# The joint of two stages: piece order, issuing queue and scale engine in the hand-over from a 7x7 convolution to an MLP

## The chip, the cores and the metric

One NeuronCore of a Trainium2 chip runs the whole kernel. The metric is device time in microseconds (us), as the median of repeated runs; a profiled execution of the same kernel gives the lines shown. Engines: PE is TensorE, DVE is VectorE, ACT is ScalarE, POOL is GpSimd, SP is SyncE, which here only issues DMAs.

## The reference

Two blocks with a residual each, on x of 8 x 96 x 96 x 192 in float32. The second, which the change is about, is a group norm, a 7x7 depthwise convolution, a norm over the 192 channels and an MLP of 192 to 768 to 192.

```python
def reference(x, ...):
    # layer 0: projection to 384, 3x3 depthwise conv, four running means, norm, projection to 192
    x = x + _L0_conv_ref(_gn(x), ...)
    # layer 1
    x = x + _L1_conv_ref(_gn(x), ...)
    return x

def _L1_conv_ref(x, dw_kernel, dw_bias, ln_gamma, ln_beta, w0, b0, w1, b1, gamma):
    y = lax.conv_general_dilated(x, dw_kernel, ...) + dw_bias      # 7x7, one filter a channel
    mu = jnp.mean(y, axis=-1, keepdims=True)
    var = jnp.mean(jnp.square(y - mu), axis=-1, keepdims=True)
    y = (y - mu) * lax.rsqrt(var + EPS) * ln_gamma + ln_beta
    y = jax.nn.gelu(jnp.einsum('bhwc,cd->bhwd', y, w0) + b0, approximate=False)
    return (jnp.einsum('bhwd,dc->bhwc', y, w1) + b1) * gamma
```

## The kernel before

Stages a to c compute layer 0 and leave its result in DRAM as `X1_d`. The change is in the last two stages.

**Stage d, the convolution.** The work is cut into 32 blocks, `todo[n]`: two halves of the batch times 16 groups of 12 channels (`NI` is 16). For a block, `load_raw(n, t)` fetches three tiles (`t` is 0 to 2) of 384 KB twice from `X1_d` (L926), `load_band(n)` fetches the filter bands (L936), `scale_steps(n)` applies the group norm in 24 small steps (`scale`, L951 to L960: on ScalarE or VectorE, by `n` and `t`) and one copy of the band to the other half of the partitions (`spread`, L964). `conv_d(n, c)` does one of six columns: 24 matmuls in the trace (L1337) and two evictions with the bias by ScalarE (L1347). `store_d(n)` writes the block to `Y_d` with six DMAs of SP (L1364 to L1369). The first `N1` = 19 blocks run one after the other in stage d proper ("own" blocks, 0 to 18). The last 13 (19 to 31) are *inlaid*: their steps are put into the slots of stage e.

**Stage e, norm and MLP.** It runs over 36 tiles of rows, `load_y(n)`, each of which gives two *units* u (72 units). A tile comes in 40 pieces: for each of eight partition blocks `q` four main pieces `b` of 60 KB (L1398) and one small piece of 16 KB with the channels of the last group (L1404). `q` below 4 goes to the buffer `ya`, the rest to `yb`; there are two buffers of each, so tile 2 needs the place of tile 0. The norm of a unit is a chain of seven steps, `norm_steps_e(u)`: sums, mean, center, square (ScalarE), squares, powers (a pow on GpSimd, L1508), scale, nearly all of the rest on VectorE. Three transposes (`turn_in`, L1529) hand it to TensorE; `first_layer` (L1544, L1554) and its GELU on ScalarE (L1563), `second_layer` (L1574), the residual add on VectorE (`xo`, L1585) and the output DMA by GpSimd (L1593) follow. `load_r` fetches the residual rows of a tile (1.5 MB, L1419), `bias_r` adds a bias to them on GpSimd (L1425).

**Order.** All of it is written out by hand: each engine executes its instructions in the order in which the program names them. In the own blocks the loop over `n` names: loads of block n + 2, store of block n - 1, `steps`, the six columns (with two pieces of tile 0 after each, on ScalarE's queue, in blocks 12 to 14: `main_y`), then `on_scalar` and `rest_y`. Tile 0's other pieces are named at the end of block 16 (`NI`), tile 1 at the end of block 17. The chain of unit 0 begins in block 17, that of unit 1 in block 18. In the loop over units the chain of unit u + 2 and the rest of unit u + 1's are named between the parts of unit u; `slot()` is called five times a unit, and names one slot of inlaid work and up to 14 pieces of a tile that is being loaded. A tile n + 2 is loaded from the end of unit 2n on.

**Semaphores.** DMAs of SP and ScalarE share eight semaphores in turn, those of GpSimd another eight; in the built program a DMA waits for the one that had the same semaphore before it, and besides for whatever it depends on by its data.

Of the kernel before, what the change touches and what calls it, by code (L numbers as in the profile page):

```python
# [101 lines left out]
def conv_blocks_kernel(  # L102
# [31 lines left out]
    nc = tc.nc  # L134
# [30 lines left out]
    NH = B // 2  # L165
# [85 lines left out]
    with ExitStack() as ph:  # L251
# [258 lines left out]
        with tc.manual_schedule():  # L510
# [7 lines left out]
            bn, last, cols = stats_a(0)  # L518
# [5 lines left out]
            for b in range(B):  # L524
                more = b + 1 < B
                for t in range(n_t):
                    u = b * n_t + t

                    n, j = divmod(u - 2, NJ)
# [3 lines left out]
                    if t == 0 and more:  # L533
                        bn, last, nxt_cols = stats_a(b + 1)
# [47 lines left out]
    NI = len(place)  # L582
# [254 lines left out]
    NI = D // GC  # L837
# [53 lines left out]
    NT = 3  # L891
# [7 lines left out]
    N1 = NI + 3  # L899
# [3 lines left out]
    def load_raw(n, t, eng=None):  # L903

        hf, i = todo[n]
        if n >= N1 and t == NT - 1:
            pool, bufs = d_pools[2], 1
        elif n >= N1 or ((n == 0 or n % 2) and t < NT - 1):
            pool, bufs = early, NT - 1
        elif n == 0 or n % 2:  # L910
            pool, bufs = gp, 1
        else:
            pool, bufs = d_pools[1], NT
        raw = pool.tile([128, NH, NV, GC, WQ], F32, tag="raw", name="raw", bufs=bufs)
        raws[n, t] = raw
        row = NGC * NV * GC * WQ
        run = NV * GC * WQ
        x1 = X1_d[hf]
        engs = (nc.sync, nc.gpsimd) if n < 2 else (eng or nc.gpsimd,) * 2
        for g, eng in enumerate(engs):  # L920
            src = bass.AP(
                tensor=x1.tensor,
                offset=x1.offset + (2 * t + g) * HG * PH * row + i * run,
                ap=[[row, 64], [ROWS * row, NH], [1, run]],
            )
            eng.dma_start(  # L926
                raw[g * 64 : (g + 1) * 64].rearrange("q b a c v -> q b (a c v)"), src
            )
# [16 lines left out]
    def scale_steps(n):  # L945

        hf, i = todo[n]
        steps = []

        def scale(t, k, b):  # L950
            if n not in xins:  # L951
                make_xin(n)
            c = slice(k * GS, (k + 1) * GS)
            sc, sh = (s1[:, hf, b, e, 2 * i + k : 2 * i + k + 1] for e in range(2))
            to = xins[n][:, t, b, c].rearrange("q c (a v) -> q a c v", a=NV)
            of = raws[n, t][:, b, :, c]
            if n == 1 or n >= N1 or (n == N1 - 1 and t):
                nc.scalar.activation(to, of, AF.Identity, bias=sh, scale=sc)  # L958
            else:
                nc.vector.tensor_scalar(to, of, sc, sh, ALU.mult, ALU.add)  # L960

        def spread():
            g, band = i % 2, bands[n]
            nc.vector.tensor_copy(  # L964
                band[(1 - g) * 64 : (2 - g) * 64], band[g * 64 : (g + 1) * 64]
            )

        for t in range(NT):
            for b in range(NH):
                for k in range(2):  # L970
                    steps.append(lambda t=t, k=k, b=b: scale(t, k, b))
        return steps + [spread]
# [72 lines left out]
    with ExitStack() as ph:  # L1045
# [172 lines left out]
        steps, stores, first_d = [], [], []  # L1218
        with tc.manual_schedule():
# [15 lines left out]
            for u in range(n_u + 1):  # L1235
# [39 lines left out]
                if held is not None:  # L1275
                    n, v = divmod(u - 1, WQ)
# [99 lines left out]
    def load_y(n):  # L1376

        hf, p, a, j = place(n)
        y = [part[(NJ3 - 1 - j) * PH + PH - 1 - p :: NJ3 * PH] for part in Y_d[hf]]
        assert CK // GS == YG  # L1380
        main = CK // GS
        cut = main * GS * WQ

        def begin():
            ya[n] = ip.tile([128, NH, CK, WQ], F32, tag="ya", name=f"ya_{n}")
            yb[n] = ip.tile([128, NH * CK * WQ + HV], F32, tag="yb", name=f"yb_{n}")
            nc.gpsimd.memset(yb[n][2 * CK :, NH * CK * WQ :], 0.0)

        def piece(q, b, eng):
            if q < 4:  # L1390
                chunk, dst = q, ya[n][q * CK : (q + 1) * CK].rearrange("i b c v -> i b (c v)")
            else:
                chunk, at = 4 + q % 2, HV if q < 6 else 0
                dst = yb[n][(q - 4) * CK : (q - 3) * CK, at : at + NH * CK * WQ].rearrange(
                    "i (b n) -> i b n", b=NH
                )
            if b < NH:
                eng.dma_start(  # L1398
                    dst[:, b, :cut].rearrange("i (g n) -> i g n", g=main),
                    y[chunk][:, :, b, a],  # L1400
                )
            else:
                g, c = divmod(chunk * (CK - main * GS), GS)
                eng.dma_start(  # L1404
                    dst[:, :, cut:],
                    y[-1][:, g, :, a, c * WQ : (c + CK - main * GS) * WQ],
                )

        return [begin] + [
            lambda eng=nc.sync, q=q, b=b: piece(q, b, eng)  # L1410
            for q in range(8)
            for b in range(NH + 1)
        ]

    def load_r(n, eng=nc.sync):
# [182 lines left out]
    with tc.manual_schedule():  # L1598
        with tc.tile_pool(name="d_own", bufs=1, side="right", **by_tile) as own:
            d_pools[1] = own  # L1600
            make_xin(1)
            load_band(2)
            make_yo(1)
            norms = norm_c(1, bank)
            y_0, y_1 = load_y(0), load_y(1)
            main_y = {
                NI - 4: [y_0[1 + q * 5 + b] for q in (0, 1) for b in range(NH)],
                NI - 3: [y_0[1 + q * 5 + b] for q in (2, 3) for b in range(NH)],
                NI - 2: [y_0[1 + q * 5 + b] for q in (4, 6) for b in range(NH)],
            }  # L1610
            rest_y = {
                NI - 5: y_0[:1],
                NI: [y_0[1 + q * 5 + b] for q in (5, 7) for b in range(NH)]
                + [y_0[1 + q * 5 + NH] for q in range(8)],
                NI + 1: y_1,
            }
            for n in range(N1):
                if n + 2 < N1:
                    for t in range(NT):
                        load_raw(n + 2, t)  # L1620
                    if n:
                        load_band(n + 2)
                if n:
                    store_d(n - 1)
                if n >= 3 and norms:
                    norms.pop(0)()
                if n == 10:
                    make_weights(bank())
                steps = scale_steps(n + 1) if n + 1 < N1 else []
                last, on_scalar = [], []  # L1630
                if n == NI + 1:
                    chain = norm_steps_e(0)
                    per_t = len(steps) // NT
                    on_scalar = steps[per_t:-1]
                    steps = steps[-1:] + chain[:3] + steps[:per_t]
                    on_scalar.insert(per_t, chain[3])
                    chain = chain[4:]
                elif n == NI + 2:
                    nxt = norm_steps_e(1)
                    steps = chain[:2] + nxt[:3] + chain[2:]  # L1640
                    on_scalar = nxt[3:4]
                    chain = nxt[4:]
                for step in steps:
                    step()
                for c in range(GS):
                    conv_d(n, c)
                    for step in main_y.get(n, [])[2 * c : 2 * c + 2]:
                        step(nc.scalar)
                for step in on_scalar + rest_y.get(n, []):
                    step()  # L1650
            store_d(N1 - 1)
            load_band(N1)
            for t in range(NT - 1):
                load_raw(N1, t)
# [7 lines left out]
        slots, after = [], []  # L1662
        for n in range(N1, len(todo)):
            more = n + 1 < len(todo)
            scales = scale_steps(n)
            per_t = len(scales) // NT
            slots += [after + scales[:per_t], scales[per_t : 2 * per_t], scales[2 * per_t :]]
            if more:
                for t in range(NT):
                    slots[t - 3].append(lambda n=n, t=t: load_raw(n + 1, t, nc.scalar))  # L1670
            slots += [[lambda n=n, c=c: conv_d(n, c, ps_y)] for c in range(GS)]
            if more:
                slots[-1].append(lambda n=n: load_band(n + 1, nc.scalar))
            after = [lambda n=n: store_d(n)]
# [3 lines left out]

        def slot():

            if slots and u >= 2:
                for step in slots.pop(0):
                    step()
            for step in loads[:14]:
                step()
            del loads[:14]
# [8 lines left out]
        for u in range(n_u + 1):  # L1695
            n, t = divmod(u, per)
# [87 lines left out]
```

## Time and profile before

| | |
|---|---|
| median of 3 runs | 5495.28 us (5494.1 to 5501.23) |
| profiled execution, device time | 5491.53 us |
| its span | 5489.7 us |
| its mean granted TensorE clock | 0.982 |
| own blocks of stage d | about 2560 to 2951 us |
| first matmul of unit 0 | 2950.96 us |
| first inlaid column (unit 2) | 3065.98 us |
| DMAs from SP and ScalarE (hardware queues) | 44.2% and 3.4% of 16 engines' span |
| DMAs from GpSimd (software queue) | 18.2% |

The profile page gives busy time by engine, the span in slices, the chain that ended last and the costliest groups. A line of time reads: start, duration, engine, source line, operation, out<-in, shape, count, and in brackets the idle time of that engine before it with what ended it. A line of the table of stretches reads: stretch, its length, busy us of PE, PE weight load, DVE, ACT and POOL with instruction counts, granted clock, DMA share, GB/s.

### The profile page before, as it was taken

How to read it: one execution, taken by the hardware profiler on the slowest of the kernel's cores; microseconds unless marked ns; L12 is line 12 of the kernel's file. 1: busy time of each engine (PE TensorE's matmuls, PEld its weight loads, DVE VectorE, ACT ScalarE, POOL GpSimd, SP SyncE). 2: the span in 40 equal slices, each digit the busy share in tenths (PEclk: the TensorE clock that was granted, in tenths of full speed). 3: DMA queues.
4: the chain of work that ended last, by engine and by line, in shares of the span. 5: the costliest groups of instructions: out<-in, count | busy, mean ns of one | idle time of the engine just before them, and what ended most of it. 6: DMA issues, size and time to landing. Idle time of an engine off the chain costs nothing. (4 is left out here: it accounts for less than half of the span.)

```text
span 5489.7 us, 108072 instructions
## 1 busy us (share of the span) xinstructions
PE 5298.0 (97%) x42206; PEld 3359.4 (61%) x42206; DVE 3450.2 (63%) x6706; ACT 2593.6 (47%) x5781; POOL 2366.2 (43%) x2063
## 2 busy tenths in 40 slices
PE   6999999999999999999787899999999999999999
PEld 4666643333333899899454566666666676666767
DVE  6556539999999455555556455555566666656654
ACT  2444447777777566566434444444433233333332
POOL 1211128888888555555322232322233333333332
PEclk9999979999999999999898999999999999999999
DMA  7999869999998899899996454555433233333231
GB/s 222 285 288 276 245 179 244 243 243 244 246 242 230 247 293 293 260 287 315 290 294 171 117 136 124 131 137 137 111 90 80 79 79 80 88 91 84 79 79 41
DMA packets 793486, 1015.35 MB, mean 185 GB/s; under 512 B 331191, under 2 KB 668320, under 8 KB 790928
## 3 DMA queue, kind: packets, MB, share of 16 engines
q1 hardware_dynamic: 677000, 634.43, 44.2%
q0 software_dynamic: 84304, 331.93, 18.2%
q10 hardware_dynamic: 31672, 42.08, 3.4%
q8 instruction: 333, 5.46, 0.4%
q14 instruction: 177, 1.45, 0.1%
HBM read 603.70 MB, written 420.03 MB: 186 GB/s over the span
## 5 line engine op out<-in xcount | busy, mean ns | idle before, releaser
L1574 PEld LDWEIGHTS hp<-w1g,g 128*128 128x128 f32 x6912 | 1117.9, 190 | 140.7 <-issue 75.8
L1574 PE MATMUL hp<-w1g,g 128*128 128x192 f32 x6912 | 1174.9, 329 | 0.0
L1563 ACT ACTIVATE g<-hp,b0g 128x512 f32<-128x512 f32 x864 | 520.2, 693 | 1211.3 <-PE hp L1554 1188.0
L1593 POOL DMA_DIRECT2D out_dram<-xo x288 | 211.6, 735 | 1574.4 <-DVE xo L1585 1480.7
L1585 DVE TENSOR_TENSOR xo<-hp,r 128x384 f32<-128x384 f32 x288 | 229.0, 795 | 992.9 <-PE hp L1574 987.9
L1544 PE MATMUL hp<-yT,w0w 128*128 128x512 f32 x1728 | 780.6, 598 | 20.3 <-DVE yT L1529 20.3
L1141 PE MATMUL po<-wc,mt 128*128 128x193 f32 x3456 | 686.7, 334 | 7.4 <-DVE x1c L1175 7.1
L688 PE MATMUL pl<-pin,band 34*32 34x380 f32 (+1 forms) x13824 | 640.2, 497 | 6.2 <-DMA pin<-PL_d 4.0
L775 POOL TENSOR_TENSOR mo<-mo,z 128x768 f32<-128x768 f32 x285 | 592.5, 2079 | 5.7 <-ACT mo L713 1.6
L1141 PEld LDWEIGHTS po<-wc,mt 128*128 128x128 f32 x3456 | 555.7, 191 | 39.4 <-ACT mean L1160 31.0
L1544 PEld LDWEIGHTS hp<-yT,w0w 128*128 128x128 f32 x1728 | 321.5, 191 | 380.9 <-issue 346.2
L721 DVE TENSOR_TENSOR_SCAN z<-decay,loc 128x768 f32<-128x768 f32 x288 | 506.0, 1757 | 64.7 <-ACT loc L697 36.3
L1337 PE MATMUL hp<-xin,band 63*64 63x372 f32 (+1 forms) x4608 | 422.8, 503 | 95.2 <-ACT yo L1347 35.6
L730 DVE TENSOR_TENSOR_SCAN z<-decay,z 128x768 f32<-128x768 f32 x288 | 498.5, 1731 | 0.1
L688 PEld LDWEIGHTS pl<-pin,band 34*32 34x32 f32 x13824 | 234.1, 108 | 394.1 <-issue 390.1
L1508 POOL TENSOR_TENSOR rs<-tot,neg_half 32x32 f32<-32x32 f32 x72 | 394.8, 5483 | 122.3 <-DVE tot L1506 121.0
L709 PE MATMUL pa<-loc,mix 128*32 128x384 f32 x3456 | 439.4, 500 | 0.0
L712 PE MATMUL pa<-last,down 96*32 96x384 f32 x1152 | 434.2, 500 | 1.0 <-ACT mo L713 1.0
L1554 PE MATMUL hp<-yT,w0w 64*128 64x512 f32 x1728 | 419.5, 611 | 0.0
L1347 ACT ACTIVATE yo<-hp,dwb 128x384 f32<-128x384 f32 x384 | 197.6, 585 | 435.6 <-PE hp L1337 272.8
L697 ACT COPY loc<-pl 128x384 f32<-128x384 f32 x576 | 248.6, 484 | 312.7 <-PE pl L688 312.7
L395 PE MATMUL pm<-xT,win 128*128 128x384 f32 x1152 | 391.7, 490 | 0.0
(155 smaller groups left out, 7248.1 us busy)
## 6 DMA issues: line engine op xcount, KB each, us to landing
P<-po POOLq DMA_DIRECT2D x96, 1152.0 KB, 9.5
pin<-P SPq DMA_DIRECT2D x190, 576.0 KB
mt<-M SPq DMA_DIRECT2D x192, 384.0 KB
xq<-in_x_dram SPq DMA_DIRECT2D x96, 576.0 KB
xr<-in_x_dram SPq DMA_DIRECT2D x192, 288.0 KB
X<-x1c SPq DMA_DIRECT2D x144, 384.0 KB
out_dram<-xo POOLq DMA_DIRECT2D x288, 192.0 KB, 2.5
r<-X SPq DMA_DIRECT2D x35, 1536.0 KB
```

The lines of the kernel that those rows point to most:

```text
L688: nc.tensor.matmul(pls[g][at * RB : (at + 1) * RB, :, lo:hi], band[rows, c, kh, :], pin[rows, c, :, NJ - 1 - j, lo + kh - 1 : hi + kh - 1] ...
L709: nc.tensor.matmul(pa[at], mix[:, i, at], loc[:, q], start=True, stop=True)
L712: nc.tensor.matmul(pa[at], down[:, to], last[:, q], start=True, stop=True)
L721: nc.vector.tensor_tensor_scan(zf, decay_f, loc.rearrange("p q n -> p (q n)"), 0.0, ALU.mult, ALU.add)
L730: nc.vector.tensor_tensor_scan(zr, decay_f, zr, 0.0, ALU.mult, ALU.add)
L775: eng.tensor_tensor(m, m, z, ALU.add)
L1141: nc.tensor.matmul(po, mt[:, m, j * 128 : (j + 1) * 128], wc[:, m], start=(m == 0), stop=(m == NC - 1),)
L1337: nc.tensor.matmul(pys[g][k * 64 : (k + 1) * 64, :, lo:hi], band[rows, k * GS + c, d * ZS : d * ZS + 64], xin[rows, :, :, k * GS + c, lo + ...
L1544: nc.tensor.matmul(hps[m, q], w0w[:, 0, m * 128 : (m + 1) * 128], yT[:, 2 * q], start=True, stop=False,)
L1554: nc.tensor.matmul(hps[m, q], w0w[p, 1, m * 128 : (m + 1) * 128], yT[p, 1], start=False, stop=True,)
L1563: nc.scalar.activation(g[:, m, q], hps[m, q], AF.Gelu, bias=b0g[:, m : m + 1], scale=1.0)
L1574: nc.tensor.matmul(po[:, q], g[:, m, q, k * 128 : (k + 1) * 128], w1g[:, m], start=(m == 0), stop=(m == NE - 1),)
```

## The change

Five things are changed, all between block 16 and unit 3 except the first, which holds for every tile.

1. The pieces of a tile are named with `b` outside and `q` inside, so the small pieces come last. The lists for tile 0 are written for that order and hold the same pieces.
2. Some pieces go to GpSimd's queue: the small ones of tiles 0, 1 and 2, the main ones of `q` = 7 of tile 1, and of `q` = 3 and 7 of tile 2.
3. The last own block, 18, is scaled on VectorE alone (before: its tiles 1 and 2 on ScalarE), and all 24 steps and the band copy are named ahead of the sums, mean and center of unit 0. The square and what follows of unit 0, and the sums, mean and center of unit 1, are named after column 2 of block 18 (`between`); the square of unit 1 comes after block 18's columns.
4. The raw tiles of block 20 are loaded by GpSimd (before: ScalarE), those of later blocks by ScalarE as before.
5. Slots of inlaid work are taken from unit 1 on (before: unit 2).

```diff
-            if n == 1 or n >= N1 or (n == N1 - 1 and t):
+            if n == 1 or n >= N1:
                 nc.scalar.activation(to, of, AF.Identity, bias=sh, scale=sc)
...
+        def engine(q, b):
+            if n < 3 and (b == NH or q % 4 == 3 and n and q >= 11 - 4 * n):
+                return nc.gpsimd
+            return nc.sync
+
         return [begin] + [
-            lambda eng=nc.sync, q=q, b=b: piece(q, b, eng)
+            lambda eng=engine(q, b), q=q, b=b: piece(q, b, eng)
+            for b in range(NH + 1)
             for q in range(8)
-            for b in range(NH + 1)
         ]
...
-                last, on_scalar = [], []
+                between, last = [], []
                 if n == NI + 1:
                     chain = norm_steps_e(0)
-                    per_t = len(steps) // NT
-                    on_scalar = steps[per_t:-1]
-                    steps = steps[-1:] + chain[:3] + steps[:per_t]
-                    on_scalar.insert(per_t, chain[3])
-                    chain = chain[4:]
+                    steps += chain[:3]
+                    chain = chain[3:]
                 elif n == NI + 2:
                     nxt = norm_steps_e(1)
-                    steps = chain[:2] + nxt[:3] + chain[2:]
-                    on_scalar = nxt[3:4]
+                    between = chain[:3] + nxt[:3] + chain[3:]
+                    last = nxt[3:4]
                     chain = nxt[4:]
...
                     for step in main_y.get(n, [])[2 * c : 2 * c + 2]:
                         step(nc.scalar)
-                for step in on_scalar + rest_y.get(n, []):
+                    if c == 2:
+                        for step in between:
+                            step()
+                for step in last + rest_y.get(n, []):
                     step()
...
-                    slots[t - 3].append(lambda n=n, t=t: load_raw(n + 1, t, nc.scalar))
+                    slots[t - 3].append(lambda n=n, t=t: load_raw(n + 1, t, nc.scalar if n > N1 else None))
...
-            if slots and u >= 2:
+            if slots and u >= 1:
```

More of the change, by code (lines that the diff above doesn't have):

```diff
@@ L1606, in conv_blocks_kernel @@
             main_y = {
-                NI - 4: [y_0[1 + q * 5 + b] for q in (0, 1) for b in range(NH)],
-                NI - 3: [y_0[1 + q * 5 + b] for q in (2, 3) for b in range(NH)],
-                NI - 2: [y_0[1 + q * 5 + b] for q in (4, 6) for b in range(NH)],
+                NI - 4: [y_0[1 + b * 8 + q] for q in (0, 1) for b in range(NH)],
+                NI - 3: [y_0[1 + b * 8 + q] for q in (2, 3) for b in range(NH)],
+                NI - 2: [y_0[1 + b * 8 + q] for q in (4, 6) for b in range(NH)],
             }
@@ L1612, in conv_blocks_kernel @@
                 NI - 5: y_0[:1],
-                NI: [y_0[1 + q * 5 + b] for q in (5, 7) for b in range(NH)]
-                + [y_0[1 + q * 5 + NH] for q in range(8)],
+                NI: [y_0[1 + b * 8 + q] for q in (5, 7) for b in range(NH)]
+                + y_0[1 + NH * 8 :],
                 NI + 1: y_1,
```

## The prediction

> **What bounds the kernel now.** I read the page first, then the table of stretches, then TensorE's line of time, then the other engines around each hole.
>
> ```profile
> PE 5298.0 (97%) x42206; PEld 3359.4 (61%) x42206; DVE 3450.2 (63%) x6706; ACT 2593.6 (47%) x5781; POOL 2366.2 (43%) x2063
> ```
> ```profile
> 2900.00:3000.00 100.00, 66.22 (x520) 40.63 (x511) 59.43 (x139) 45.93 (x78) 26.53 (x11) 0.83 0.67 167
> 3000.00:3100.00 100.00, 81.36 (x407) 51.26 (x407) 51.46 (x104) 35.29 (x60) 23.16 (x15) 0.90 0.51 121
> 3100.00:3200.00 100.00, 100.00 (x570) 63.59 (x567) 50.30 (x98) 48.75 (x84) 31.13 (x15) 1.00 0.52 129
> ```
>
> TensorE is the bound: only 192 us of the span are not covered by it. The change touches nothing before about 2905 us, and from 3100 us on TensorE is full. So what can be won lies in 2900 to 3100, where 33.8 + 18.6 = 52.4 us are idle. TensorE's line of time shows where:
>
> ```profile
> 2909.53 15.86 PE L1337 MATMUL hp<-xin,band 63*64 63x384 f32 x192 [1.31 <-ACT yo L1347]
> 2937.53 13.50 PE L1337 MATMUL hp<-xin,band 63*64 63x384 f32 x144 [12.15 <-DVE T L1447]
> ...
> 2987.08 2.04 PE L1544 MATMUL hp<-yT,w0w 128*128 128x512 f32 x2 [18.58 <-DVE yT L1529]
> 2990.28 5.46 PE L1544 MATMUL hp<-yT,w0w 128*128 128x512 f32 x6 [1.15 <-DVE yT L1529]
> ...
> 3065.98 4.04 PE L1337 MATMUL hp<-xin,band 63*64 63x384 f32 x24 [18.64 <-DVE band L964]
> ```
>
> Three holes, G1 (12.15), G2 (18.58) and G3 (18.64). What ends each is read off VectorE and the queues:
>
> ```profile
> 2924.93 1.87 DVE L1481 TENSOR_REDUCE s<-ya 128x32 f32<-128x1024 f32 x1 [12.15 <-DMA yb<-Y]
> 2934.32 3.60 ACT L958 ACTIVATE xin<-raw,s 128x192 f32<-128x192 f32 x8
> 2938.49 5.45 POOL L1508 TENSOR_TENSOR rs<-tot,neg_half 32x32 f32<-32x32 f32 x1 [47.24 <-DVE tot L1506]
> 2979.14 1.01 DVE L1481 TENSOR_REDUCE s<-yb 128x16 f32<-128x512 f32 x1 [18.70 <-DMA yb<-Y]
> 3052.71 1.00 DVE L1481 TENSOR_REDUCE s<-yb 128x16 f32<-128x512 f32 x1 [19.08 <-DMA yb<-Y]
> ```
>
> G1: block 18 waits for its scales, which stand on VectorE and ScalarE behind the sums of unit 0, and those wait for the last rows of tile 0 (2924.93). G2: the scale of unit 1 stands on VectorE behind the sums of unit 2, which wait for tile 1. G3: the band copy of the first inlaid block stands behind the sums of unit 4, which wait for tile 2. The queue of SP shows why tile 1 is late:
>
> ```profile
> 2934.48 2.97 SPq L1398 DMA_DIRECT2D ya<-Y  x4
> 2941.54 1.87 SPq L1398 DMA_DIRECT2D ya<-Y  x4
> 2946.34 2.38 SPq L1398 DMA_DIRECT2D yb<-Y  x4
> 2965.52 0.30 SPq L1404 DMA_DIRECT2D yb<-Y  x1
> ```
>
> Until 2946 a piece takes about 0.47 us; then raw blocks and residual rows (3.8 MB, issued by GpSimd from 2943.90) fill the DMA engines, and the next piece goes at 2965.5.
>
> **What the Trainium skill says.** "DMA: Bandwidth & Descriptors", section "Issuing engines are not separate DMA queues": DMAs of all issuers share 16 engines, so another issuer saves only its issue time. The 16.8 us wait above agrees. "SBUF — State Buffer", section "SBUF: two separate sides": GpSimd can't write descriptors while VectorE holds the shared port. The trace doesn't show this: GpSimd issued raw blocks in 0.62 us each beside VectorE's scales, so I charge nothing. "TensorE: Matmul & The Clock Gate", part 1: an idle array falls to half clock. The trace agrees (granted clock 0.50 in 2975 to 2990, and 4.04 us for 24 matmuls after G3 against 2.12 later).
>
> **The change, part by part.**
>
> *Own scales on VectorE, sums after them.* VectorE is free at 2907.8 (24 scales of block 17 done), block 16 releases its xin at about 2913.5; 24 scales took 7.05 us, the band copy 1.46: ready at 2922.5, before block 17 ends on TensorE (2925.4). G1 closes for the convolution. Sums of unit 0 then start near 2924.9 as before. But block 18 ends earlier only to wait for unit 0, whose chain isn't earlier; so G1 is moved, not won.
>
> *Small rows of tile 0 by GpSimd.* Eight issues of about 0.7 us leave SP. The yb ones wait in the built program for SP's main pieces of tile 0; with SP's last at 2921.3 they land near 2926.7, as the old ones did. Won here: SP goes on to the store of block 16 at 2921.3 instead of 2925.2. A store of a block held SP 9.2 us (2925.21 to 2934.43), so tile 1 starts at 2930.6.
>
> *Tile 1: 28 pieces on SP, 12 on GpSimd.* The first eight took 6.1 us (2934.48 to 2940.58); 20 more at 0.47 to 0.51: 9.7. Last issue 2946.4; landing 1.7 us later (small rows issued until 2923.2 let the reduce start at 2924.93): 2948.1. The raw blocks can't collide: they stand on GpSimd behind tile 1.
>
> *The wait that this adds.* The built program lets the last small yb rows of tile 1 on GpSimd wait for SP's last main pieces, and the power of unit 0 (5.45 us) is queued behind them, with the raw blocks and residual rows behind that. Two issues after 2948.1, at 0.62: the power runs 2949.3 to 2954.8, against 2938.5 to 2943.9. The scale of unit 0 starts at 2954.85 instead of 2946.05. Its 3.6 us, three transposes (2.9): squares of unit 1 at 2961.35 against 2954.92 (which had itself waited 2.39 us for ScalarE); 6.4 later, so the power of unit 1 ends at 2963.9 + 6.4 = 2970.3. Now tile 1 is there, so the scale of unit 1 starts at 2970.3 instead of 2980.06. **Won at G2: 9.8 us** of 18.6; what is idle instead is a hole of about 20 us ahead of unit 0.
>
> *Square of unit 0 between blocks' columns.* On ScalarE after column 2 of block 18, whose evictions wait for the store of block 16 (landed near 2935): about 2938.3 to 2941.4. The power could start at 2945 then; covered by the 2949.3. Bare, this path gives a scale at 2952.6 (VectorE does the sums of unit 1 first), only 2.2 us better.
>
> *Tile 2, inlay from unit 1.* SP's stores of blocks 17 and 18 (9.2 and 10.2 us) and the band end by about 2970. Tile 2 needs its buffer free: transposes of unit 1, near 2980. 24 pieces then take 11 to 15 us instead of sharing with 16 others and the residual rows until 3048; the last small rows by GpSimd come between 3008 and 3018 (raw blocks of 12.6 us landing ahead of them on its eight semaphores). Unit 2 starts at 3024.4 - 9.8 + 4.2 (two inlaid columns of 2.12 us, now in unit 1) = 3019, and VectorE may be held until about 3035 before PSUM runs out. The band copy now comes in unit 1, ahead of the sums of unit 4. **G3 closes: 18.64 + 1.92 + 0.35** (slow matmuls: 4.04 - 2.12, 4.05 - 3.70) = 20.9. ScalarE's three scale groups (3.63 each) end near 3004, TensorE reaches the inlay near 3006: cover of 2 us; without it, a microsecond or two.
>
> *Nothing from:* raw blocks of block 20 on GpSimd (ScalarE loses 6 issues of 0.64 us, off the path), order of pieces in later tiles (TensorE full), inlay one unit earlier as such (the same matmuls).
>
> **Sum:** 9.8 + 20.9 = 30.7. Profiled execution: span 5489.7, device time 5491.5; becomes 5459.0 and 5460.8. It lies 3.8 below the median shown, 5495.3; from that: 5464.6, forecast **5465**.
>
> **Rivals.**
> 1. *GpSimd in order chokes in unit 1.* It gets 16 pieces of tile 2, six raw blocks, outputs, a bias and powers; eight in flight, each round as slow as a raw block (12.6): three rounds after 2991 reach 3029, outputs and power stand behind, TensorE stalls 15 to 20 us. For: one in-order queue with waits on ScalarE. Against: the median landing of outputs was 2.5 us. Gain 11 to 16: 5479 to 5484. Chance 0.17.
> 2. *Slower: tile 1 holds GpSimd.* Unlike before, its lateness now delays even unit 0. Every issue waits for the one eight places before; if landings take as long as those of raw blocks (13.0 median), a piece costs 13.0 / 8 = 1.6 us, and 28 of them from 2930.6, with landing and two issues, put the power at 2978. All is given back when it starts at 2949.3 + 30.7 = 2980: from about 1.66 us a piece on, the whole is slower; at 2.0 the power starts at 2989.5, and 5495.3 + 9.5 = 5505. Against: nothing large moves while tile 1 loads. Chance 0.12.
> 3. *GpSimd isn't held* (small rows early, stores quick): power at 2939, G2 closes by 17.9 and all gives 38.8: 5456. The waits in the program speak against it. Chance 0.1.
> 4. *No effect*, G3 merely moved by as much as G2 gives: 0.04.
>
> The forecast itself, 5457 to 5474: 0.57. A measurement tells about 0.2% (11 us) from no change. Faster 0.83, same 0.06, slower 0.11. Range 5453 to 5484: it leaves out the slower rival and the edges.
>
> **What would show it.** Block 18 following block 17 with no hole; one hole of about 20 us ahead of the first matmul of unit 0, which starts near 2960; power of unit 0 on GpSimd near 2949, behind rows of tile 1; unit 1 following unit 0 with under 6 us lost; no hole at the first inlaid column, near 3006. I am wrong if the power comes after 2960, if sums of unit 4 hold TensorE, or if stalls appear after 3100.

## The result, and the profile after

The changed kernel took 5455.61 us (median of 6 runs, 5448.79 to 5470.68) beside 5494.4 us for the kernel before in the same session (6 runs): ratio 0.9948, 95% interval 0.9932 to 0.9963. That is 20 to 37 us less, 29 at the middle of the interval. The profiled execution has a span of 5453.2 us against 5489.7. The same stretches as before, in the changed kernel (stretch, its length, busy us of PE, weight load, DVE, ACT, POOL with counts, granted clock, DMA share, GB/s):

```profile
2900.00:3000.00 100.00, 74.84 (x526) 43.89 (x518) 73.59 (x168) 52.09 (x88) 45.86 (x44) 0.86 0.77 208
3000.00:3100.00 100.00, 98.98 (x560) 59.44 (x560) 56.40 (x97) 44.08 (x77) 36.95 (x29) 1.00 0.52 123
```

TensorE was idle for 52.4 us in these 200 us before and is idle for 26.2 now, and its clock is full from 3000 us on. Its line of time after, only the lines with idle time ahead of them:

```profile
2907.04 29.62 PE L1337 MATMUL hp<-xin,band 63*64 63x384 f32 x336 [4.10 <-ACT yo L1347]
2956.07 5.77 PE L1549 MATMUL hp<-yT,w0w 128*128 128x512 f32 x8 [19.42 <-DVE yT L1534]
2976.91 1.10 PE L1549 MATMUL hp<-yT,w0w 128*128 128x512 f32 x2 [0.99 <-ACT sq L1501]
2978.20 1.98 PE L1549 MATMUL hp<-yT,w0w 128*128 128x512 f32 x4 [0.20 <-ACT g L1568]
3001.02 2.13 PE L1337 MATMUL hp<-xin,band 63*64 63x384 f32 x24 [1.47 <-DVE band L964]
```

(After L1404 the line numbers are 5 higher than before.) The first line is 336 matmuls in one piece: G1, between blocks 17 and 18, is gone. A new hole of 19.42 us stands ahead of unit 0. Of G2 1.19 us are left ahead of unit 1, and of G3 1.47 at the first inlaid column, which is now in unit 1. What ends the new hole is read off GpSimd's line of time after:

```profile
2923.73 1.63 POOL L1404 DMA_DIRECT2D ya<-Y  x3 [0.87 <-DMA yb<-Y]
2942.87 2.27 POOL L1404 DMA_DIRECT2D yb<-Y  x4 [17.51 <-DMA yb<-Y]
2945.21 6.10 POOL L1513 TENSOR_TENSOR rs<-tot,neg_half 32x32 f32<-32x32 f32 x1
```

GpSimd stands for 17.51 us at four small rows of tile 1, which wait for SP's main pieces. The power of unit 0 is queued behind them; VectorE had made its input by 2939.4, so it is held for 5.8 us.

**A tie point.** Traces are laid side by side at the moment when SP issues the first of tile 0's last eight main pieces (2915.32 us before, 2908.82 after), since the chain to unit 0 runs through SP's queue in both kernels. Nothing that the change is meant to touch lies ahead of it, yet in the 14 profiled executions of this study it lies anywhere from 2899.3 to 2932.3 us. That scatter is in every median. From the tie point to the end of the span it is 2574.4 us before and 2544.4 after: **30.0 us are won behind it**, of the 36.5 between the two spans. This number, one execution each, is given for the experiments too.

It has a scatter of its own. TensorE ended block 16 at 2914.0 us before and at 2913.9 after, so laid side by side there, 36.4 us are won behind. In the 14 executions TensorE's end of block 16 lies from 3.0 us ahead of SP's tie point to 5.1 behind it (1.3 ahead before, 5.1 behind in the changed kernel, which is the most of all). The interval of the medians, 20 to 37 us, holds both numbers; differences of a few us between two single executions are not told by either.

### The profile page after: what moved, and what is told of

The parts are those of the page before. It is cut to its first block, busy times and chain, and to the rows that moved or that the text cites. A ratio compares the mean times of both kernels' runs of the same rounds, so it can differ in the third digit from the quotient of the medians.

```text
span 5453.2 us, 107702 instructions
## 1 busy us (share of the span) xinstructions
PE 5283.8 (97%) x42206; PEld 3353.5 (61%) x42206; DVE 3461.5 (63%) x6722; ACT 2580.4 (47%) x5765; POOL 2387.6 (44%) x2105
## 5 line engine op out<-in xcount | busy, mean ns | idle before, releaser
L1141 PEld LDWEIGHTS po<-wc,mt 128*128 128x128 f32 x3456 | 555.8, 191 | 39.1 <-ACT mean L1160 30.5
```

The source lines that it names most:

```text
L1141: nc.tensor.matmul(po, mt[:, m, j * 128 : (j + 1) * 128], wc[:, m], start=(m == 0), stop=(m == NC - 1),)
```

## The experiments

| kernel | ratio to before (95%) | tie point to end, us | against before |
|---|---|---|---|
| changed kernel | 0.9948 (0.9932 to 0.9963) | 2544.4 | -30.0 |
| own scales alone | 0.9998 (0.9987 to 1.0009) | 2573.4 | -1.0 |
| pieces alone | 0.9937 (0.9922 to 0.9952) | 2540.5 | -33.9 |
| order alone | 0.9989 (0.9977 to 1.0002) | 2562.7 | -11.7 |
| changed, all pieces on SP | 0.9950 (0.9933 to 0.9967) | 2549.4 | -25.0 |
| changed, old order | 0.9957 (0.9945 to 0.9970) | 2553.0 | -21.4 |
| changed, tile 2 on SP | 0.9947 (0.9928 to 0.9967) | 2547.0 | -27.4 |
| the same, slots from unit 2 | 0.9946 (0.9930 to 0.9962) | 2544.5 | -29.9 |
| changed, small rows of tile 1 late | 0.9958 (0.9936 to 0.9980) | 2543.7 | -30.7 |
| changed, tile 1 on SP | 0.9947 (0.9933 to 0.9962) | 2542.4 | -32.0 |
| the same, square first | 0.9956 (0.9939 to 0.9972) | 2543.9 | -30.5 |
| changed, bias on VectorE | 0.9934 (0.9916 to 0.9952) | 2542.8 | -31.6 |
| tile 1 on SP, bias on VectorE | 0.9953 (0.9935 to 0.9971) | 2536.0 | -38.4 |

The theory at the start, A, is the prediction's: G1 is only moved, G2 is won by taking SP's pieces off its way, G3 closes because tile 2 comes in time.

**1. Own scales alone** (part 3 of the change, put into the kernel before; the diffs of this section are cut to the lines that matter).

```diff
-            if n == 1 or n >= N1 or (n == N1 - 1 and t):
+            if n == 1 or n >= N1:
...
+                    steps += chain[:3]
...
+                    between = chain[:3] + nxt[:3] + chain[3:]
```

> The kernel before with the third change alone (block 18 scaled on VectorE, the norm steps of units 0 and 1 renamed around column 2). Theory A (the first hole is moved, not won, and what pays is when tile 1 arrives): no hole between blocks 17 and 18, but unit 0 starts some 10 us later than before, since the square of unit 0 now stands on ScalarE behind evictions that wait for the store of block 16; the power of unit 0 comes later, the raw blocks behind it too, tile 1 loads undisturbed, so the hole ahead of unit 1 falls from 18.6 to under 6 us; the hole at the first inlaid column stays at 18 to 19. Sum 8 to 12 us faster than before. Theory B (the first hole is won for good by this part): 12 us faster with unit 0 starting 12 us earlier and both later holes as before.

Nothing was won. TensorE's line of time in this run:

```profile
2930.39 6.96 PE L1337 MATMUL hp<-xin,band 63*64 63x384 f32 x48 [6.81 <-ACT yo L1347]
2951.30 6.26 PE L1544 MATMUL hp<-yT,w0w 128*128 128x512 f32 x8 [13.96 <-DVE yT L1529]
2977.92 2.04 PE L1544 MATMUL hp<-yT,w0w 128*128 128x512 f32 x2 [7.34 <-DVE yT L1529]
...
3058.34 4.01 PE L1337 MATMUL hp<-xin,band 63*64 63x384 f32 x24 [19.89 <-DVE band L964]
```

The holes are in other places but sum to 49.2 us with the 1.15 of unit 1's second part (51.1 before). G1 is moved, as predicted: what is left of it, 6.81, lies inside block 18, and 13.96 now stand ahead of unit 0. The 8 to 12 us that I expected all the same did not come: I had let tile 1 load undisturbed, but the raw blocks were issued in the middle of it and VectorE waited 11.56 us for it.

**2. Pieces alone** (parts 1 and 2: order and GpSimd as second issuer; scales, raw blocks and slots as before).

```diff
+        def engine(q, b):
+            if n < 3 and (b == NH or q % 4 == 3 and n and q >= 11 - 4 * n):
+                return nc.gpsimd
+            return nc.sync
...
+            for b in range(NH + 1)
             for q in range(8)
-            for b in range(NH + 1)
```

> The kernel before with the first and second change alone (order of pieces, pieces by GpSimd). Theory A: the hole between blocks 17 and 18 stays near 12, a second hole of 8 to 12 us opens ahead of unit 0 because the power waits on GpSimd for tile 1 (it starts 6 us or more after its input is ready), the hole ahead of unit 1 falls under 4, and the one at the first inlaid column goes to under 4: in all within 3 us of the changed kernel, about 25 to 28 us faster than before. Theory B (the scales are what wins the first hole): 12 us slower than the changed kernel, so 16 us faster than before.

As fast as the whole change (the two intervals overlap): nothing shows that parts 3 to 5 add to it. TensorE's line of time:

```profile
2932.86 13.43 PE L1337 MATMUL hp<-xin,band 63*64 63x384 f32 x144 [15.80 <-DVE T L1452]
2952.22 5.94 PE L1549 MATMUL hp<-yT,w0w 128*128 128x512 f32 x8 [5.93 <-DVE yT L1534]
...
3028.80 2.13 PE L1337 MATMUL hp<-xin,band 63*64 63x384 f32 x24 [0.85 <-DVE band L964]
```

G1 is still there (15.80 us), the hole ahead of unit 0 is 5.93 instead, and at the inlay, which here starts in unit 2, 0.85. So G3 needs neither slots from unit 1 nor raw blocks on GpSimd, *if* the pieces are shared.

**3. Order alone** (part 1; every piece still on SP).

```diff
         return [begin] + [
             lambda eng=nc.sync, q=q, b=b: piece(q, b, eng)
-            for q in range(8)
             for b in range(NH + 1)
+            for q in range(8)
         ]
```

> The kernel before, with one part of the change: each tile's pieces named block by block with the small rows last, all still on SyncE; own scales, inlay and slots as before. Theory B: what makes tiles 1 and 2 late before is that a small row, written beside main pieces of the same buffer, waits on SyncE until those have landed, and in the old order four such waits stand between the main pieces of each tile (2946.3 to 2977.3 and 3016.6 to 3048.5 us). With the small rows last there is one wait instead of four, tile 1 is issued before the raw blocks fill the transfers, and the hole at the first inlaid column is under 4 us. The first hole (12 us between the last two own blocks) stays, and the hole ahead of unit 1 becomes small: time 5455 to 5466 us. Rival: a second issuer or the moved scales are needed as well; then VectorE still waits over 10 us for tile 1 or tile 2 and the time is 5475 us or more.

My theory B fell: the order alone isn't enough. Tile 1 comes sooner (VectorE waits 11.00 us for it, 18.70 before), but G3 stays at 15.85 us:

```profile
3057.20 3.80 PE L1337 MATMUL hp<-xin,band 63*64 63x384 f32 x24 [15.85 <-DVE band L964]
```

The reason isn't the one that I had given. The two longest waits of SP from 2985 to 3060 us in this run (line, waited for, us in total, times, longest):

```profile
SPq L1404 <- DMA raw<-X: 20.4, 3, 16.7
SPq L1398 <- DVE yT L1529: 16.5, 1, 16.5
```

and in the kernel before:

```profile
SPq L1398 <- DMA raw<-X: 13.4, 1, 13.4
SPq L1404 <- DMA yb<-Y: 11.2, 4, 5.2
...
SPq L1404 <- DMA raw<-X: 1.4, 1, 1.4
```

A piece of tile 2 has no data to do with a raw block. It waits for one because the two have the same semaphore. The program names ScalarE's six raw issues of block 20 in unit 2, behind all of tile 2's pieces; but the built program deals out the eight semaphores of SP and ScalarE in an order of its own, and there most of the six lie among tile 2's last thirteen pieces. So in this run SP had issued the last main piece by 3017.0 us and waited with the first small row for a raw block that ScalarE issued 12 us later:

```profile
3011.68 5.33 SPq L1398 DMA_DIRECT2D yb<-Y  x4
3029.07 1.28 ACTq L926 DMA_DIRECT2D raw<-X  x2
3033.74 3.07 SPq L1404 DMA_DIRECT2D ya<-Y  x4
```

(The other wait, 16.5 us for the transposes yT that free the buffer, lies ahead of tile 2's first piece.) ScalarE issues its raw blocks only between its scales of block 19, here in the kernel before:

```profile
3031.43 3.64 ACT L958 ACTIVATE xin<-raw,s 128x192 f32<-128x192 f32 x8
3035.09 1.28 ACTq L926 DMA_DIRECT2D raw<-X  x2
3036.48 3.63 ACT L958 ACTIVATE xin<-raw,s 128x192 f32<-128x192 f32 x8 [1.41 <-issue]
3040.14 1.25 ACTq L926 DMA_DIRECT2D raw<-X  x2
```

and SP's next pieces follow behind:

```profile
3024.99 15.07 SPq L1398 DMA_DIRECT2D yb<-Y  x4
3042.00 0.30 SPq L1404 DMA_DIRECT2D yb<-Y  x1
3042.35 1.87 SPq L1398 DMA_DIRECT2D yb<-Y  x4
3048.20 0.30 SPq L1404 DMA_DIRECT2D yb<-Y  x1
```

That the transfers were not the limit is seen in the same 18 us, 3024 to 3042, in 40 slices (busy tenths of the DMA engines, then GB/s): in 17 of the 40 nothing moves.

```profile
DMA  0001245400000004875001000002769999963439
GB/s 0 0 0 25 53 114 132 122 0 0 0 0 0 0 0 164 273 256 181 0 0 36 0 0 0 0 0 24 102 205 341 208 249 236 201 126 73 118 32 82
```

This gives theory D, which was drawn from these waits after all runs, so no expectation names it: G3 closes when SP's pieces of tile 2 no longer stand behind ScalarE's raw blocks. Either the raw blocks go to GpSimd, whose DMAs have eight semaphores of their own (part 4), or the late pieces do (part 2).

**4. The changed kernel with all pieces on SP.**

```diff
-            if n < 3 and (b == NH or q % 4 == 3 and n and q >= 11 - 4 * n):
+            if n < 0 and b == NH:
                 return nc.gpsimd
```

> The changed kernel with no piece on GpSimd: the small rows of all tiles stand last, but every piece of tiles 0 to 2 is issued by SyncE. Theory A: the 8 small rows of tile 0 then stand again ahead of the store of block 16 (3.9 us of SyncE in the kernel before), so ScalarE's squares, the power of unit 0 and tile 1 come about 4 us later than with tile 0's small rows alone on GpSimd; the power is not held by GpSimd, as in the run with tile 1 all on SyncE, so unit 0 is within 4 us of the changed kernel's. Time 5455 to 5466 us: most of the gain needs no GpSimd. Rival: GpSimd as a second issuer is what the gain comes from; then the three holes sum to 40 us or more and the time is 5480 to 5496 us.

Unit 0 came no later than in the changed kernel, 43.9 us behind the tie point beside 47.3, since no row of tile 1 held the power on GpSimd (it starts 0.1 us behind its input); the hole at the first inlaid column was 0.86. So with parts 3 to 5 in place the gain doesn't need GpSimd as second issuer: this run's tie-point time is 5 us longer, and the ratios, 0.9950 and 0.9948, don't differ. The Trainium skill, "DMA: Bandwidth & Descriptors", section "Issuing engines are not separate DMA queues", says that another issuer saves only issue time; this run agrees. Runs 2 and 3 differ from it: there the raw blocks stay on ScalarE, and the second issuer is worth 22 us by the tie point (0.9937 beside 0.9989), most of it at G3 (0.85 beside 15.85), where it takes the late pieces away from the shared semaphores.

**5. The changed kernel in the old order** (small rows between main pieces, but still on GpSimd).

```diff
+            for q in range(8)
             for b in range(NH + 1)
-            for q in range(8)
```

> The changed kernel with the pieces of every tile named in the old order (small rows between the main pieces), but the small rows and the share of the main pieces of tiles 0 to 2 on GpSimd as in the change. Theory B: SyncE then issues main pieces of tiles 0 to 2 alone and has no small row to wait at; the waits are GpSimd's. Time and holes as in the changed kernel: 5450 to 5462 us, hole at the first inlaid column under 4 us. Either cure is enough. Rival: the order of the main pieces matters by itself, or the small rows of later tiles on SyncE, which stand between main pieces again, stall TensorE behind unit 4; then the time is 5466 us or more.

5461.6 us, at the upper edge of what I expected; 3.36 us at the inlaid column. The order adds about 9 us by the tie point (21.4 against 30.0), though the intervals of the two ratios overlap. What the trace shows directly: GpSimd now waits four times for tile 1's rows (18.11, 1.57, 1.31 and 5.40 us), the power of unit 0 is held for 13.2 us behind its input (5.8 in the changed kernel), and the hole ahead of unit 0 is 27.47.

**6. Tile 2 on SP, and 7. the same with slots from unit 2.** These cross what is left for G3.

```diff
-            if n < 3 and (b == NH or q % 4 == 3 and n and q >= 11 - 4 * n):
+            if n < 2 and (b == NH or q % 4 == 3 and n and q >= 11 - 4 * n):
```

> The changed kernel, with all 40 pieces of tile 2 named on SyncE's queue and none on GpSimd's. Theory A: the third hole (18.64 us at the first inlaid column before, 1.47 after) closed because SyncE reaches tile 2 sooner, not because tile 2 is shared: its pieces start when unit 1's transposes have freed the buffer, and 40 of them at 0.47 us are issued in about 19 us. So the hole at the first inlaid column stays under 5 us and the time is that of the changed kernel or up to 3 us more: 5454 to 5462 us. Rival: the share on GpSimd is what brings tile 2 in time; then VectorE waits for tile 2 ahead of the inlaid blocks' scaling, the hole is back at 10 us or more, and the time is 5465 to 5476 us.

```diff
-            if slots and u >= 1:
+            if slots and u >= 2:
```

> The changed kernel with tile 2 all on SyncE and with the inlaid blocks' slots from the third unit again, so neither of the two parts of the change that touch tile 2 and the inlay directly. It crosses the runs that took away one of them. Theory A (tile 2 is in time because SyncE reaches it about 10 us sooner): the last small rows of tile 2 land 3 to 8 us after VectorE wants them, and the hole at the first inlaid column is 2 to 8 us; time 5455 to 5466 us. Theory C (either part closes the third hole, and one of them is needed): VectorE waits 12 us or more for tile 2 ahead of the inlaid block's scaling, the hole is 12 to 18 us, and the time is 5466 to 5480 us.

The hole at the inlay is 2.52 us in the first and 0.85 in the second, below even what theory A gave it. TensorE's line there and, as above, all waits of SP from 2985 to 3060 us, in the second run:

```profile
3045.78 2.12 PE L1337 MATMUL hp<-xin,band 63*64 63x384 f32 x24 [0.85 <-DVE band L964]
```
```profile
SPq L1398 <- DVE yT L1534: 50.5, 2, 31.4
SPq L1404 <- DMA r<-X: 2.6, 1, 2.6
```

No wait for a raw block is left, and VectorE takes up the sums of unit 4 without waiting. (The 50.5 us are SP waiting for buffers to come free; nobody waits for it.) SP issued the last row of tile 2 18 us before GpSimd issued the first raw block:

```profile
3013.27 1.85 SPq L1404 DMA_DIRECT2D yb<-Y  x4
3032.91 1.30 POOL L926 DMA_DIRECT2D raw<-X  x2 [2.84 <-ACT xin L958]
```

In run 3 SP was 12 us ahead of the raw blocks and still had to wait for them. The size of the third hole in every arrangement that was run, in us:

| | raw blocks of block 20 on ScalarE | on GpSimd |
|---|---|---|
| tile 2 all on SP | 18.64 (before), 19.89, 15.85 | 0.86, 2.52, 0.85 |
| its small rows and a share on GpSimd | 0.85 | 1.47 (changed), 3.36, 6.14 (residual rows late, below), 0.85 in four others |

Neither the own scales (moved in the 19.89) nor the slots (from unit 2 in the last 0.85 of the upper row) sort these numbers; the place of the raw blocks and of tile 2 does. Both theories of the last expectation fall: C, because neither of its two parts was there and the hole is closed all the same; A, because nothing was late at all. Theory D fits all of them. It stays open in one respect: part 4 put alone into the kernel before was not run. All runs of the right-hand column contain part 3, and part 1 or the small rows on GpSimd; that the raw blocks' place is enough without these is not shown.

**8 to 10. The hole ahead of unit 0.** Three ways to shorten it: name tile 1's small rows behind unit 0's power; put tile 1 all on SP; and besides, name unit 0's squares ahead of block 18's first column and its scaling ahead of unit 1's centring.

```diff
-                NI + 1: y_1,
+                NI + 1: y_1[: 1 + NH * 8],
...
-                    between = chain[:3] + nxt[:3] + chain[3:]
+                    between = chain[:3] + y_1[1 + NH * 8 :] + nxt[:3] + chain[3:]
```

> The changed kernel with the eight small rows of tile 1 named after the power of unit 0 on GpSimd's queue. Theory A (the power is held by these rows): the power starts within 0.5 us of its input (VectorE's variance), 5 to 6 us earlier than in the changed kernel; unit 0 starts 4 to 5 us earlier, the hole of 19.4 falls to about 15, since VectorE's sums of unit 1 stand ahead of the scale; unit 1 is ready earlier by 2 to 4 us; in all 2 to 4 us faster than the changed kernel. Rival (the hole is set by the sums of unit 0 or by ScalarE alone): the hole stays at 19 to 20 us.

```diff
-            if n < 3 and (b == NH or q % 4 == 3 and n and q >= 11 - 4 * n):
+            if n in (0, 2) and (b == NH or q % 4 == 3 and n and q >= 11 - 4 * n):
```

> The changed kernel with all 40 pieces of tile 1 on SP. Theory A: the power of unit 0 isn't held and starts 5 to 6 us earlier; tile 1 issues for about 20 us from the store of block 16 on and is through when the raw blocks start, so the hole ahead of unit 1 doesn't come back (under 5 us): equal to the changed kernel or up to 4 us faster. Rival (tile 1 must be split over two queues): the last pieces meet the raw blocks as before, VectorE waits for tile 1 for 10 us or more, and 8 to 15 us of the gain are lost.

```diff
-                    between = chain[:3] + nxt[:3] + chain[3:]
+                    between = chain[:3] + nxt[:2] + chain[3:] + nxt[2:3]
...
                 for c in range(GS):
+                    if c == 0:
+                        for step in between:
+                            step()
                     conv_d(n, c)
```

> The run with tile 1 all on SyncE, and in addition unit 0's squares named ahead of block 18's first column on ScalarE and VectorE (they stood after its third column), and unit 0's scaling named ahead of unit 1's centring. The squares then don't queue behind evictions that wait for the store of block 16 (about 3 us), and the scaling doesn't queue behind two applies (about 2 us). Theory A: the hole ahead of unit 0 falls from 14.0 us to 8 to 10; behind it VectorE is nearly without idle time (20 to 23 us busy in each 26), so of these 5 us about 3 are kept at unit 3: 5449 to 5454 us beside 5456 for the changed kernel. Rival: behind unit 0 the transfer of tile 1 and of the residual rows sets the time; then unit 0 starts earlier, units 1 and 2 wait as much longer, and the time is that of the changed kernel within 1 us.

All three did what they should ahead of unit 0: the power starts 0.1 us behind its input instead of 5.8, and unit 0's first matmul comes 7.4, 7.6 and 8.9 us earlier behind the tie point than in the changed kernel, so the hold of the power is real. And all three gave it back: from unit 0's first matmul to unit 3's it is 106.6, 106.0 and 109.2 us, beside 99.9 in the changed kernel. None is faster than the changed kernel by its ratio, as the rival of the third had it. In the first, residual rows come late and the inlay waits 6.14; in the third VectorE waits 5.86 us for tile 1, now beside the raw blocks, and unit 1 stands 6.69 and 1.15. In the second it is VectorE's own work ahead of unit 1:

```profile
2978.47 5.98 DVE L1452 COPY T<-s 32x48 f32<-32x48 f32 x4
```

Four copies that take 0.75 us elsewhere (here one of the four took 5.41), beside GpSimd's bias in the same run:

```profile
2978.78 5.43 POOL L1430 TENSOR_TENSOR r<-r,b1g 128x3072 f32<-128x3072 f32 x1 [3.58 <-DMA r<-X]
```

**11 and 12. That bias on VectorE**, named ahead of the first residual add; in the changed kernel, and with tile 1 on SP.

```diff
-        bias_r(0)
...
+            if u == 1:
+                bias_r(0, nc.vector)
             second_layer(u - 1, 0, pool)
```

> The changed kernel with the bias of the first residual tile (128x3072, 5.43 us on GpSimd) computed by VectorE instead, named ahead of the first addition of the residual. Measures what GpSimd's long two-input operation costs VectorE: if VectorE's four copies of T are held by it (3.29 us in the changed kernel, 5.29 before, 0.75 elsewhere), they take 0.75 us here; the bias itself should take VectorE about 3.5 us (three times the 1.2 us of a 128x1024 two-input apply). Theory A: the two nearly cancel, and the time is that of the changed kernel within 2 us. Rival: the copies were slow because of the transfers of that time (about 260 GB/s); then they stay at 3 us or more and the time is 2 to 4 us longer.

> The run with tile 1 all on SyncE, and in addition the bias of the first residual tile on VectorE (3.34 us there) instead of GpSimd. In the run with tile 1 on SyncE VectorE's four copies of T took 5.98 us beside that bias, ahead of unit 1's transposes, and TensorE waited 3.06 and 1.50 us for these. Theory A: the copies take 0.75 us, the two waits sum to under 1.5 us, and the first inlaid column comes 2 to 4 us earlier: 5450 to 5455 us. Rival: the landing of tile 1 or of the residual rows, not the copies, decides when unit 1 can start; then the waits ahead of unit 1 stay at 3 us or more and the time is that of the changed kernel within 2 us.

The cost measured by itself, VectorE's line of time in the first of the two:

```profile
2980.20 0.75 DVE L1452 COPY T<-s 32x48 f32<-32x48 f32 x4
...
2984.54 3.34 DVE L1430 TENSOR_TENSOR r<-r,b1g 128x3072 f32<-128x3072 f32 x1
```

The copies take 0.75 us (3.29 in the changed kernel), the bias 3.34. With tile 1 on SP as well, the early unit 0 is kept: the waits ahead of unit 1 are 0.24 and 0.17 us, from unit 0's first matmul to unit 3's it is 99.3 us, and the first inlaid column comes 8.4 us earlier behind the tie point than in the changed kernel; the time from there to the end is 2452.2 us in both. By this one trace it is the best version. By the measured times it isn't shown to be: its interval, 0.9935 to 0.9971, and that of the changed kernel nearly coincide.

## Why the prediction was right, and where it was not

**The sum.** 30.7 us were predicted behind the untouched part; 30.0 were measured there from SP's tie point, 36.4 from TensorE's end of block 16. 0.9948 of 5494.4 is 5466 us, beside the forecast of 5465; the bare median of the changed kernel lies 10 us lower, inside the scatter of the tie point.

**G1, "moved, not won".** Right, and shown by two runs: own scales alone wins nothing (0.9998), and pieces alone wins all with G1 still open.

**The new wait on GpSimd.** Right in kind and place. Predicted for the power was 2949.3 to 2954.8, measured (6.5 us added to lay it on the time of before) 2951.7 to 2957.8; predicted for the hole about 20 us, measured 19.42. What I didn't see is that taking it away wins next to nothing as long as the copies, the raw blocks and the residual rows behind it are as they are (runs 8 to 10).

**The term of G2: 9.8 predicted, 7.3 measured from SP's tie point** (unit 2's first layer, two inlaid columns of 2.12 us counted in: 3024.38 before; 3014.78 + 6.5 - 4.24 after). The power came 2.4 us late: the store of block 16 held SP for 10.5 us, not 9.2, and four small rows (2.27 us of issuing), not two, stood between SP's last piece and the power. The 1.47 at the inlaid column, counted as covered, is in it too. From TensorE's end of block 16 the term measures about 14, so whether it was too large or too small is not settled.

**The term of G3 was right in size, 20.9 against 20.7, and its reason was wrong.** (From unit 2's first layer to unit 3's: 57.6 us before, 41.2 after with two more inlaid columns, 4.24. The 2.0 us between 7.3 + 20.7 and the 30.0 come behind unit 3.) I wrote that tile 2's pieces were slow from "sharing with 16 others and the residual rows until 3048", that the band copy must come ahead of the sums of unit 4, and that raw blocks on GpSimd bring nothing. The runs showed that SP stood at semaphores that ScalarE's raw blocks held, with the transfers idle for much of that time; that with the raw blocks on GpSimd the hole is closed without tile 2's share on GpSimd and the earlier slots (0.85); and that the pieces on GpSimd close it without the raw blocks (0.85). That this term came out was luck: the change contains both cures; the prediction credited one of them, tile 2's share on GpSimd, for a wrong reason, and put the other at nothing.

**The rivals.** GpSimd didn't choke in unit 1 (1.19 us idle there). Tile 1 did not hold it beyond 2951.7, far from the 2980 at which all would be given back: SP's main pieces took 15.9 us from first issue to last, 0.57 us each, not 1.66. "GpSimd isn't held" named 5456 us, which is near the median, but it is refuted by GpSimd's line of time: it was held for 5.8 us.

**A reading.** The eight small rows that left SP were put at about 0.7 us each; before, SP took 3.9 us for the eight, 0.49 each. The sum used the 3.9.

## What to carry to other kernels

When a transfer is late, look whether the DMA engines were busy meanwhile: if they stood still, the issuer was waiting, and the list of the issuer's waits names for whom. In such a program the DMAs of two engines that share semaphores are one queue for this purpose, in the order in which the built program deals them out: an issue that itself waits for computation stops a load whose pieces the program named ahead of it. And a stall that is removed on the way to the end is worth only what the next wait behind it leaves: here some 8 us at unit 0 became about 1, until the copies behind it were freed.

## What the runs showed of the hardware

GpSimd's bias, an add of 128x3072 on two inputs in SBUF, held up VectorE's copies until it ended: four copies of 32x48 took 5.98 us beside it (5.43 us), one of them 5.41 and the others 0.17 to 0.18 each, and 0.75 in all in the run where VectorE did the bias. The Trainium skill, "SBUF — State Buffer", section "SBUF: two separate sides", calls the shared port of the two an exclusive lock, held for the whole instruction, rather than a split of bandwidth; the bias agrees. The power, also a GpSimd operation on two inputs in SBUF, doesn't: the kernel before ran the four copies at their usual speed in the middle of the power of unit 0 (2938.49 to 2943.94):

```profile
2941.13 0.74 DVE L1447 COPY T<-s 32x48 f32<-32x48 f32 x4
```

So not every GpSimd operation of 5.4 us holds the copies up; why the power doesn't isn't shown. The same bias took 3.34 us on VectorE.

In the changed kernel SP took 6.26 us to issue eight pieces of 60 KB right behind a store, and 1.87 for four (0.47 each) where it went fastest; GpSimd needed 0.57 to 0.63 us for a piece of 60 KB and 0.55 for a small row.
